# Mamba scan kernel: the reverse direction's convolution diagonals move to ScalarE, the gated product behind the fourth scan

## The chip, the cores and the metric

The kernel runs on one core of one Trainium2 chip. The metric is the device time of one execution in microseconds (us). Before the change the median of three runs is 1444.02 us (1441.96 to 1447.98).

Engine names are those of the profile: PE is TensorE's matrix multiply and PEld its weight load, DVE is VectorE, ACT is ScalarE, POOL is GpSimd, and SP is SyncE, which here issues most of the DMA transfers. A line L685 is line 685 of the kernel before, unless the text says otherwise.

## The reference, cut to what matters

The input x has 2 sequences of 1024 tokens and 256 channels. A projection with low-rank additions (mixed per sequence by `cond_8`) feeds a bidirectional Mamba layer with 512 inner channels and 16 states; a masked projection and a mixture of experts (8 experts, the best 2 for each token) follow.

```python
def _selective_scan(x, dt, Bm, Cm, A, D):
    dA = jnp.exp(dt[..., None] * A)
    dBx = (dt * x)[..., None] * Bm[:, :, None, :]
    def step(h, inputs):
        dA_t, dBx_t, C_t = inputs
        h = dA_t * h + dBx_t
        y = jnp.einsum('bdn,bn->bd', h, C_t)
        return (h, y)
...
    return jnp.swapaxes(ys, 0, 1) + x * D[None, None, :]

def _mamba_dir(h, in_proj_w, conv_w, conv_b, x_proj_w, dt_proj_w, dt_proj_b, A_log, D, out_proj_w):
    xz = h @ in_proj_w.T
    x, z = (xz[..., :D_INNER], xz[..., D_INNER:])
    x = jax.nn.silu(_causal_depthwise_conv(x, conv_w, conv_b))   # 4 taps a channel
    x_dbl = x @ x_proj_w.T
    dt = jax.nn.softplus(x_dbl[..., :DT_RANK] @ dt_proj_w.T + dt_proj_b)
    Bm = x_dbl[..., DT_RANK:DT_RANK + D_STATE]
    Cm = x_dbl[..., DT_RANK + D_STATE:]
    A = -jnp.exp(A_log)
    y = _selective_scan(x, dt, Bm, Cm, A, D)
    y = y * jax.nn.silu(z)
    return y @ out_proj_w.T
out_fwd = _mamba_dir(hidden_states, ...)          # weights _f
out_rev = _mamba_dir(h_rev, ...)                  # weights _r, reversed time
x = x + out_fwd + jnp.flip(out_rev, axis=1)
x = x + ffn(cond2(x))                             # top-2 mixture of experts
```

## The kernel before

**Stages.** Channels lie on the 128 partitions, tokens along the free dimension. A short start loads weights and prepares the first block (up to 48.5 us in the profile), the scan stage runs to about 1010 us, and the mixture of experts fills the rest.

**Blocks and periods.** The scan stage has 8 blocks, each one sequence, one direction and one chunk of 512 tokens. Their order is, for each of the two sequences, forward chunk 0, forward chunk 1, reverse chunk 1, reverse chunk 0. Blocks 0, 1, 4 and 5 are forward, blocks 2, 3, 6 and 7 reverse. The direction turns from forward to reverse behind blocks 1 and 5 and back behind block 3. A block has 16 periods, counted from 0 in each block; a period handles 32 channels x 16 states, that is 128 partitions (32 channels x 4 groups of states) times 4 scans of 512 tokens.

One period j does this, and the order on each engine is the order in which the program writes it:

- DVE makes the injection dt·x·B into a new tile `hb` of 128 x 2048 (L1517; in a block's first period in four pieces, the other three at L1549), then four scans in place (L668). Blocks 0, 2, 4 and 6 start from zero, the odd ones from a saved state. `hb` has four buffers.
- ACT makes the decays exp(dt·A), one of 128 x 512 for each scan (L642). They lie in two PSUM banks, so a decay is written two scans ahead.
- POOL multiplies the whole tile with C (L685), behind the fourth scan; in even blocks it copies the end state first (L682).
- PE adds up the states (`add_states`, folds of L711): each even period it folds the two tiles before it into the bank `yp` (there is one). Ahead of a new group of four periods it writes D·x into that bank (L700) and, in reverse blocks, adds the forward direction's result (L704).
- When `yp` holds 128 channels it is taken: by ACT as a plain copy in forward blocks (L733), in reverse blocks by DVE as a product with the gate silu(z), the gated product (L731). That is so in periods 5, 9 and 13, and in period 1 of the block that follows; the very last one is behind the loop.
- In period 15 PE spreads the next block's B rows over the partitions (`broadcast_b`, L609) into a tile of four banks of which there is one. It stands in PE's order ahead of that period's other work, and the next block's injections read it.

**Background steps.** While block i is scanned, block i+1 is prepared, one step at a time, some pieces per period. For each of the four groups of 128 channels d: the input projection's xp (evicted by ACT, L359) or the gate's sz (L382), the convolution as four matrix products with diagonal weights `cdiag` (L406, evicted by ACT at L415 and turned into silu by ACT and POOL), then the projection to dt, B and C (L452), then for each d the step `delta`: a product on PE (L493), six ACT operations (L513 to L528), four on POOL (ev L531, av L534, dt L537, u L540), and two DMA writes of the rows dt and u by SP (L543, L546). SP reads these rows back for a period, spread over partitions, two periods ahead (L630). In one period ACT gets at most four of these operations ahead of its decays (`ACT_CAP`) and up to two more late in the period, POOL at most two (`POOL_CAP`), placed ahead of that period's product with C.

**The diagonals.** `cdiag` holds 16 diagonals of 128 x 128 (4 groups of channels x 4 taps), for one direction at a time: `ident` times a tap per channel (L162, `conv_diagonals`). POOL makes the first 16 in the start. When the direction of the prepared block's successor differs, the 16 of the other direction are made anew, once the last convolution of this direction is through: in blocks 0, 2 and 4. They are put behind the POOL work of the last convolution step, four at a time (one function call counts as one operation toward `POOL_CAP`):

```python
if i + 1 < nblk and order[i + 1][1] != rev:
    out[-1]["pool"] += [partial(conv_diagonals, 1 - rev, d) for d in range(KI)]
```

**The gated product's place.** In the loop over the four scans s = 0 to 3 (L1549 and on) the gated product of a reverse block is written behind the second scan, `if s == 1 and ("vec", j) in takes`; routing work and the output projection's addition to x go behind the third and fourth.

Of the kernel before, what the change touches and what calls it, by code (L numbers as in the profile page):

```python
# [13 lines left out]
AF = mybir.ActivationFunctionType  # L14
# [7 lines left out]
DI, NS, DTR, DC = 512, 16, 16, 4  # L22
# [3 lines left out]
KI = DI // P  # L26
# [6 lines left out]
NG = NS // NI  # L33
# [15 lines left out]
def bimamba_moe_kernel(  # L49
# [23 lines left out]
    nc = tc.nc  # L73
# [3 lines left out]
    ident = const.tile([P, P], F32, name="ident")  # L77
# [38 lines left out]
    dirs = []  # L116
    for tag, (conv_w, conv_b, xprojT, dtprojT, dt_b, a_log, d_skip) in (("f", dir_f), ("r", dir_r)):
        dirs.append(
            dict(
                conv_w=mconst.tile([P, KI, DC], F32, name=f"conv_w_{tag}"),  # L120
# [5 lines left out]
                d=mconst.tile([P, KI], F32, name=f"d_{tag}"),  # L126
# [31 lines left out]
    cdiag = mconst.tile([P, KI, DC, P], F32, name="cdiag")  # L158

    def conv_diagonals(rev, d):  # L160
        for k in range(DC):
            nc.gpsimd.tensor_scalar(  # L162
                cdiag[:, d, k, :], ident, dirs[rev]["conv_w"][:, d, k : k + 1], None, ALU.mult
            )


    own = dict(reuse_waits="tile")
# [158 lines left out]
    order = []  # L326
    for b in range(B):
        order += [(b, 0, c) for c in range(NCH)] + [(b, 1, c) for c in reversed(range(NCH))]
    nblk = len(order)
# [10 lines left out]
    def step(product, act=(), hold=1, vector=(), pool=(), then=()):  # L340
        return dict(
            product=product,
            act=list(act),
            hold=hold,
            vector=list(vector),
            pool=list(pool),
            then=list(then),
            ready=lambda: True,
        )
# [40 lines left out]
    def steps_prepare(i, spares={}):  # L390

        b, rev, c = order[i]
# [4 lines left out]
        out = []  # L397
# [23 lines left out]
        def silu(v, tag, counts=0):  # L421


            box = {}

            def act1():
                box["e"] = small.tile([P, TC], F32, tag=tag, name=f"silu_{tag}_{nm}")
                nc.scalar.activation(box["e"], v, AF.Exp, scale=-1.0)

            def act2():  # L430
                nc.scalar.activation(box["e"], box["e"], AF.Ln, bias=1.0)

            def act3():
                nc.scalar.activation(box["e"], box["e"], AF.Exp, scale=-1.0)

            def multiply():
                nc.gpsimd.tensor_tensor(v, v, box["e"], ALU.mult)
                blk["gated"] = blk.get("gated", 0) + counts

            return [act1, act2, act3], multiply  # L440

        def also(st, acts, multiply):
            st.setdefault("also", []).append(step(None, acts, pool=[multiply]))

        def x_proj():
            box = {}
# [114 lines left out]
        if i:  # L561

            tags = ("ev", "u", "av", "dt")
            for d, tag in enumerate(tags):
                acts, multiply = silu(xc[:, d, :], tag, 1)
# [2 lines left out]
                if rev and d in (1, 2):  # L568
                    also(out[d], *silu(szs[i][:, d - 1, :], tags[d - 1]))
            out[-1]["hold"] = len(out[-1]["act"])  # L570
        if i + 1 < nblk and order[i + 1][1] != rev:
            out[-1]["pool"] += [partial(conv_diagonals, 1 - rev, d) for d in range(KI)]
        out.append(x_proj())
        if rev:
            for d in (2, 3):
                also(out[-1], *silu(szs[i][:, d, :], tags[d]))
        out += [delta(d, spares.get(d)) for d in range(KI)]
        return out

    def step_out(i, m):  # L580

# [35 lines left out]
    def spread(j):  # L617

        i, g = divmod(j, NQ)
        rows = blocks[i]["rows"]  # L620
        assert blocks[i].get("written", 0) > g // NI, (i, g)
        out = []
        for w, tag in enumerate(("dt4", "dtx4")):
            t = ring.tile([P, TC], F32, tag=tag, name=f"{tag}_{j}")
            if j < 2 * AHEAD:

                for k in range(NI):
                    nc.sync.dma_start(t[ts(k, QW)], rows[w, ts(g, QW), :])
            else:
                nc.sync.dma_start(  # L630
                    t, rows[w, ts(g, QW), :].unsqueeze(0).to_broadcast([NI, QW, TC])
                )
            out.append(t)
        spreads[j] = out
# [589 lines left out]
    for m in FIRST_TURN:  # L1224
# [6 lines left out]
    spares = {  # L1231
        d: pair.tile([P, 4, TC], F32, tag=tag, name=f"first_dt_{d}") for d, tag in ((2, "c4"), (3, "sz"))
    }
# [4 lines left out]
    for d in FIRST_TURN[:-1]:  # L1238
        for k in range(DC):
            taps, tap = xp[:, d, ds(k, TC)], w["conv_w"][:, d, k : k + 1]  # L1240
# [223 lines left out]
    act_q, pool_q, vec_q, takes, sp_q = [], [], [], {}, {}  # L1464
# [23 lines left out]
    def next_act(j):  # L1488
        nonlocal held
        f, frees, st = act_q.pop(0)  # L1490
        f()
        held -= frees
        if st:
            after_act(j, st)
# [8 lines left out]
    for j in range(total):  # L1503
        mark = len(traced)
        i, g = divmod(j, NQ)
        if j == max(START, i * NQ):
            steps += background(i)

        for f in sp_q.pop(j, ()):
            f()  # L1510
        if j + AHEAD < total:
            spread(j + AHEAD)
        more = extra.pop(j, dict(sp=[], act=[], pe=[], vector=[], pool=[]))
        for f in more["sp"]:
            f()
        injects = inject(j)
        injects.pop(0)()  # L1517

        if ("act", j) in takes:
            act_q.insert(0, (takes.pop(("act", j)), False, None))  # L1520
        for _ in range(min(ACT_CAP, len(act_q))):
            next_act(j)
        late = [partial(next_act, j)] * min(2, len(act_q))
        for f in more["act"]:
            f()

        if g == NQ - 1 and i + 1 < nblk:
            broadcast_b(i + 1)
        if steps and (not steps[0] or not held and steps[0]["ready"]()):
            st = steps.pop(0)  # L1530
            if st:
                begin(st)
        if more["pe"]:
            late = [f() for f in more["pe"]]
        if j and g % 2 == 0:
            add_states((j - 2, j - 1))
            i0, g0 = divmod(j - 2, NQ)
            if g0 % NI == NI - 2:
                rev0 = order[i0][1]
                takes["vec" if rev0 else "act", j + 1 if rev0 else j + 2] = partial(  # L1540
                    take, i0, g0 // NI
                )
        if j + KD >= total:
            last_out(j + KD - total, range(KI - 1))

        for s in range(NG):
            scan(j, s)
            if injects:
                injects.pop(0)()  # L1549

            if s >= NG - 2 and late:
                late.pop(0)()
            decay(j + (s + 2) // NG, (s + 2) % NG)
            if s == 1 and ("vec", j) in takes:
                takes.pop(("vec", j))()
            elif s == NG - 2:
                for f in more["vector"]:
                    f()
            elif s == NG - 1 and vec_q:
                vec_q.pop(0)()  # L1560
                held -= 1
        if rest:
            act_q[0:0] = [(rest_product(n), False, None) for n in ("mm", "yp")]

        for f, st in [pool_q.pop(0) for _ in range(min(POOL_CAP if j else 2 * POOL_CAP, len(pool_q)))]:
            f()
            if st:
                after_pool(j, st)
        for f in more["pool"]:
            f()  # L1570
        readout(j)
        pin(mark)
# [293 lines left out]
```

## Time and profile before

| | |
|---|---|
| median of the runs | 1444.02 us (1441.96 to 1447.98) |
| profiled execution, its own time | 1445.72 us |
| its span, first to last instruction | 1443.9 us |
| mean granted TensorE clock | 0.88 |
| busy PE | 1166.0 us (81 %) |
| busy DVE | 1251.9 us (87 %) |
| busy ACT | 671.9 us (47 %) |
| busy POOL | 966.5 us (67 %) |

Busy time by stage, in us (the row of the scan stage is shown with the prediction):

| stage | PE | DVE | ACT | POOL | granted clock | DMA share |
|---|---|---|---|---|---|---|
| start, 0 to 48.5 | 39.53 | 28.95 | 20.18 | 19.27 | 0.88 | 0.45 |
| experts, 1010 to 1443.9 | 413.75 | 314.97 | 69.05 | 98.41 | 0.99 | 0.71 |

How to read the views: a group of instructions has its line, engine, operation, output <- inputs, shape and count, then its busy time, the mean of one in ns, and the idle time of its engine just before them with what ended most of it. A timeline row has start, duration, engine, line and operation, and in brackets the wait before it and what released it. The costliest groups of the whole run:

```profile
L685 POOL TENSOR_TENSOR hb<-hb,c 128x2048 f32<-128x2048 f32 x127 | 576.0, 4536 | 61.7 <-DVE hb L668 52.7
L711 PE MATMUL yp<-hb,fold 128*32 128x512 f32 x1024 | 308.7, 694 | 68.7 <-POOL hb L685 68.6
L668 DVE TENSOR_TENSOR_SCAN hb<-da,state,hb 128x512 f32<-128x512 f32 x256 | 310.5, 1267 | 8.5 <-DVE hb L1517 0.5
L668 DVE TENSOR_TENSOR_SCAN hb<-da,hb 128x512 f32<-128x512 f32 x256 | 294.8, 1206 | 13.4 <-ACT da L642 5.3
L1517 DVE TENSOR_TENSOR hb<-dtx,b 128x2048 f32<-128x2048 f32 (+1 forms) x128 | 277.3, 2166 | 22.6 <-PE b L609 6.4
```

The first injections of the eight blocks start at 48.53, 165.34, 280.81, 402.40, 522.83, 643.20, 758.96 and 874.78 us.

### The profile page before, as it was taken

The numbers are of one execution on the slowest core, as the hardware profiler recorded it, in microseconds if no ns is written. First come the engines' busy times: TensorE is split into PE (matmuls) and PEld (weight loads), VectorE is DVE, ScalarE is ACT, GpSimd is POOL, SyncE is SP. The second block draws the span as 40 slices with busy tenths as digits, with TensorE's granted clock in tenths as the row PEclk, the third lists the DMA queues.
The fourth block names the chain that finished last, engine by engine and source line by source line (L and its number), as shares of the span: only waits on it lengthen the run. The fifth ranks groups of instructions, "written<-read, shape, count | busy, mean of one in ns | idle before, by whom it ended". The sixth has DMA issues, their size and how long they took to land.

```text
span 1443.9 us, 12413 instructions
## 1 busy us (share of the span) xinstructions
PE 1166.0 (81%) x3362; PEld 494.1 (34%) x3362; DVE 1251.9 (87%) x1479; ACT 671.9 (47%) x1078; POOL 966.5 (67%) x580
## 2 busy tenths in 40 slices
PE   7786776776787788677679668657999999999995
PEld 4421221221232122122123223221465656555564
DVE  6799899998999999989999998998376888888882
ACT  3666676676655665657766673332311111111110
POOL 3599998999996897999898897687222222222221
PEclk9798788798799799889778877877999999999998
DMA  5543322322322322232232244325688887921697
GB/s 146 137 126 114 108 108 77 123 106 81 106 107 72 116 104 80 84 125 90 89 130 88 82 149 152 107 91 193 217 282 287 274 289 247 313 40 22 209 336 246
DMA packets 121623, 211.32 MB, mean 146 GB/s; under 512 B 14928, under 2 KB 60240, under 8 KB 120528
## 3 DMA queue, kind: packets, MB, share of 16 engines
q1 hardware_dynamic: 110176, 199.78, 40.9%
q0 software_dynamic: 7200, 9.97, 3.4%
q10 hardware_dynamic: 4176, 0.77, 0.3%
q8 instruction: 27, 0.44, 0.1%
q14 instruction: 44, 0.36, 0.1%
HBM read 212.45 MB, written 29.49 MB: 168 GB/s over the span
## 4 chain that ended last, share of the span: by engine, by line
PE 36%; DVE 32%; POOL 21%; issue 7%; ACT 1%; DMA 1%; SPq 1%; DVEq 0%; POOLq 0%; ACTq 0%
DVE hb L668 19%; POOL hb L685 13%; PE pA L1582 9%; DVE hb L1517 9%; PE pB L1582 9%; PE pO L1661 8%; PE yp L711 4%; POOL cdiag L162 2%; PE b L609 1%; POOL ev L531 1%; PE pX L763 1%; POOL dt L537 1%; POOL u L540 1%; POOL av L534 1%; DMA yrows<-y,index 1%
## 5 line engine op out<-in xcount | busy, mean ns | idle before, releaser
L685 POOL TENSOR_TENSOR hb<-hb,c 128x2048 f32<-128x2048 f32 x127 | 576.0, 4536 | 61.7 <-DVE hb L668 52.7
L711 PE MATMUL yp<-hb,fold 128*32 128x512 f32 x1024 | 308.7, 694 | 68.7 <-POOL hb L685 68.6
L668 DVE TENSOR_TENSOR_SCAN hb<-da,state,hb 128x512 f32<-128x512 f32 x256 | 310.5, 1267 | 8.5 <-DVE hb L1517 0.5
L668 DVE TENSOR_TENSOR_SCAN hb<-da,hb 128x512 f32<-128x512 f32 x256 | 294.8, 1206 | 13.4 <-ACT da L642 5.3
L1517 DVE TENSOR_TENSOR hb<-dtx,b 128x2048 f32<-128x2048 f32 (+1 forms) x128 | 277.3, 2166 | 22.6 <-PE b L609 6.4
L642 ACT ACTIVATE da<-dt,a_r 128x512 f32<-128x512 f32 x256 | 176.0, 689 | 191.5 <-DVE hb L668 191.4
L1665 POOL DMA_INDIRECT yrows<-y,index x37 | 59.4, 1605 | 288.5 <-ACT y L1663 275.2
L642 ACT ACTIVATE da<-dt,a_f 128x512 f32<-128x512 f32 x256 | 176.4, 690 | 139.0 <-DVE hb L668 137.3
L1647 DVE STREAM_TRANSPOSE hT<-h 32x256 f32<-32x256 f32 x480 | 208.8, 435 | 6.2
L711 PEld LDWEIGHTS yp<-hb,fold 128*32 128x32 f32 x1024 | 68.0, 124 | 307.5 <-issue 167.4
L406 PE MATMUL pcv<-xp,cdiag 128*128 128x512 f32 x224 | 111.3, 642 | 26.7 <-ACT xc L415 15.9
L1586 DVE TENSOR_TENSOR h<-h,pB 128x512 f32<-128x512 f32 x73 | 50.0, 685 | 76.6 <-PE pB L1582 76.5
L1585 ACT ACTIVATE h<-pA 128x512 f32<-128x512 f32 x73 | 43.6, 597 | 146.4 <-PE pA L1582 146.3
L1663 ACT COPY y<-pO 128x256 f32<-128x256 f32 x37 | 13.8, 373 | 177.8 <-PE pO L1661 177.8
L1582 PE MATMUL pA<-w,xs 128*128 128x512 f32 x192 | 90.5, 593 | 0.2 <-DVE xs L1627 0.2
L1582 PE MATMUL pB<-w,xs 128*128 128x512 f32 x192 | 90.2, 592 | 0.0
L1661 PE MATMUL pO<-w,hT 128*128 128x256 f32 x384 | 86.9, 379 | 0.0
L334 PE MATMUL pz<-xT,in_eff 128*128 128x512 f32 x64 | 46.1, 860 | 39.9 <-ACT ev L516 39.9
L406 PEld LDWEIGHTS pcv<-xp,cdiag 128*128 128x128 f32 x224 | 43.0, 202 | 95.7 <-issue 48.3
L1661 PEld LDWEIGHTS pO<-w,hT 128*128 128x128 f32 x384 | 71.2, 190 | 9.2 <-issue 0.5
L531 POOL TENSOR_TENSOR ev<-ev,u 128x512 f32<-128x512 f32 x29 | 36.8, 1269 | 26.0 <-ACT u L528 26.0
L1582 PEld LDWEIGHTS pB<-w,xs 128*128 128x128 f32 x192 | 36.5, 190 | 45.9 <-issue 45.9
(337 smaller groups left out, 1506.5 us busy)
## 6 DMA issues: line engine op xcount, KB each, us to landing
w<-in_w_dram SPq DMA_DIRECT2D x78, 1024.0 KB
dt<-rows SPq DMA_DIRECT2D x124, 256.0 KB
dtx<-rows SPq DMA_DIRECT2D x124, 256.0 KB
xp<-in_w_dram SPq DMA_DIRECT2D x24, 1024.0 KB
in_eff<-in_w_dram SPq DMA_DIRECT2D x12, 1024.0 KB
c<-crow SPq DMA_DIRECT2D x32, 256.0 KB
rows<-dt SPq DMA_DIRECT2D x29, 256.0 KB
rows<-u SPq DMA_DIRECT2D x29, 256.0 KB
```

The source lines that it names most:

```text
L406: nc.tensor.matmul(box["ps"], cdiag[:, d, k, :], xp[:, d, ds(off, TC)], start=(k == 0), stop=(k == DC - 1),)
L531: nc.gpsimd.tensor_tensor(box["ev"], box["ev"], box["u"], ALU.subtract)
L642: nc.scalar.activation(da, spreads[j][0], AF.Exp, scale=a[:, g, s : s + 1])
L668: nc.vector.tensor_tensor_scan(h_s, das.pop((j, s))[:, ::turned], h_s, 0.0 if i % NCH == 0 else states[b, rev][:, g, s : s + 1], ALU.mult, ...
L685: nc.gpsimd.tensor_tensor(hb, hb, blocks[i]["c4"], ALU.mult)
L711: nc.tensor.matmul(yp[ts(q, QW), :], fold, hbs[j][:, s, :], start=False, stop=(s == NG - 1), tile_position=(0, q * QW), skip_group_check=True,
L1517: injects.pop(0)()
L1582: nc.tensor.matmul(ps, xs[:, k, :], w_sb[:, k, ts(n, TC)], start=(k == 0), stop=(k == KD - 1))
L1586: nc.vector.tensor_tensor(h, h, pb, ALU.mult)
L1647: nc.vector.transpose(hT[ts(k, QW), :, ts(i, QW)], hk[ts(i, QW), :, ts(k, QW)])
L1661: nc.tensor.matmul(po, hT[:, k, :], w2_sb[:, k, :], start=(k == 0), stop=(k == KH - 1))
L1665: nc.gpsimd.indirect_dma_start(out=yrows, out_offset=bass.IndirectOffsetOnAxis(ap=index_of[ph][:, k : k + 1], axis=0), in_=y, in_offset=No ...
```

## The change

Two edits. The 48 diagonals of the three turns are no longer made by POOL with a multiplication but by ACT, as an activation (identity function, the tap as its scale per channel). They no longer follow the last convolution: four of them are put into ACT's order with the step `delta` of the same d, as an additional step that begins in the same period as that `delta`'s product and is queued behind its six operations. The 16 diagonals of the start stay on POOL. And the gated product of reverse blocks is written behind the fourth scan of its period rather than behind the second; the third scan's routing work is no longer an alternative to it. `also` takes any number of POOL operations now, none included, and is called with none for the diagonals.

```diff
+    def turn_diagonals(rev, d):
+        for k in range(DC):
+            tap = dirs[rev]["conv_w"][:, d, k : k + 1]
+            nc.scalar.activation(cdiag[:, d, k, :], ident, AF.Identity, scale=tap)
...
-        def also(st, acts, multiply):
-            st.setdefault("also", []).append(step(None, acts, pool=[multiply]))
+        def also(st, acts, *pool):
+            st.setdefault("also", []).append(step(None, acts, pool=pool))
...
-        if i + 1 < nblk and order[i + 1][1] != rev:
-            out[-1]["pool"] += [partial(conv_diagonals, 1 - rev, d) for d in range(KI)]
         out.append(x_proj())
...
-        out += [delta(d, spares.get(d)) for d in range(KI)]
-        return out
+        deltas = [delta(d, spares.get(d)) for d in range(KI)]
+        if i + 1 < nblk and order[i + 1][1] != rev:
+            for d in range(KI):
+                also(deltas[d], [partial(turn_diagonals, 1 - rev, d)])
+        return out + deltas
...
-            if s == 1 and ("vec", j) in takes:
+            if s == NG - 1 and ("vec", j) in takes:
                 takes.pop(("vec", j))()
-            elif s == NG - 2:
+            if s == NG - 2:
                 for f in more["vector"]:
                     f()
             elif s == NG - 1 and vec_q:
```

In the built kernel each turn's diagonals stand on ACT four at a time, ahead of a period's third decay (its first two are written in the period before). The periods are 13 and 15 of block 0 and 1 and 3 of block 1; 10, 12 and 14 of block 2 and 0 of block 3; 10, 12 and 14 of block 4 and 0 of block 5. The eviction of the step that follows (sz, L382, or xp, L359) stands behind them. The orders of PE and SP are the same as before. On POOL 48 instructions are gone, and one product of a gate's silu stands one period earlier in block 2.

## The prediction

> **What bounds the kernel now.** The busy time by stretch comes first. Columns: PE, PEld, DVE, ACT and POOL busy us with counts, granted TensorE clock, DMA share, GB/s.
>
> ```profile
> 48.50:1010.00 961.50, 712.77 (x1825) 222.01 (x1824) 908.02 (x730) 582.69 (x920) 848.81 (x471) 0.83 0.33 109
> ```
>
> In the scan stage DVE works 908 of 961.5 us and POOL 849: two engines close to full in one loop, and each can hold the other. The time that a change can win here is DVE's idle time, so I read next what DVE waits for (total us, times, longest).
>
> ```profile
> DVE ysum L731 <- PE yp L711: 9.8, 5, 3.9
> ...
> DVE hb L668 <- ACT da L642: 5.6, 6, 2.3
> ```
>
> Five gated products (L731) wait 9.8 us for TensorE's folds. In the timeline they start at 354.88, 385.85, 505.11, 888.31 and 986.35, after waits of 3.88, 2.86, 1.93, 0.48 and 0.69 us. The other eleven wait for nothing.
>
> For what the diagonals do, I read the chain of waits around the first turn of direction (start, us, what).
>
> ```profile
> 127.98 3.50 POOL cdiag L162 x6
> ...
> 138.76 4.53 POOL hb L685
> 143.29 1.22 POOL ev L531
> ...
> 153.38 4.57 POOL hb L685
> 157.95 0.04 issue
> 158.00 3.62 PE yp L711 x14
> 161.62 2.34 PE b L609 x5
> ...
> 165.34 0.70 DVE hb L1517
> ```
>
> Sixteen diagonals put POOL behind, its products with C stay late, TensorE's fold of periods 12 and 13 waits for product 13, the new block's B row waits behind the fold in TensorE's order, and DVE's first injection of block 1 waits for B. In the timeline injections stand 6.85 us apart (120.45, 127.30, 134.15, 141.00); from 141.00 on that puts block 1 at 161.55. It starts at 165.34: 3.8 us lost.
>
> **The change, part by part.** *Removed from POOL:* 48 diagonals, 16 at each of three turns (blocks 0, 2 and 4).
>
> ```profile
> L162 POOL TENSOR_SCALAR cdiag<-ident,conv_w_r 128x128 f32<-128x128 f32 x32 | 18.7, 606 | 0.0
> ```
>
> 48 x 0.606 = 29.1 us of POOL work go. That is not the gain: each turn wins only until the next thing in the loop is late.
>
> Turn 1 (block 0). POOL's next step, ev of the first dt, starts at 143.25 behind the late product. Its input u ends on ACT at 140.66 + 0.61 = 141.27, and ev stands before product 12 in POOL's order. So POOL can come forward by at most 143.25 - 141.27 = 2.0 us. From there to the end of product 13 it works without a pause, so product 13 ends at about 156.0 instead of 157.94. Fold and B keep their 7.4 us (157.94 to 165.34): block 1 starts at about 163.4. Gain 1.9 of the 3.8.
>
> Turn 3 (block 4) is the same with a longer delay:
>
> ```profile
> 593.93 0.61 ACT L528 ACTIVATE u<-u 128x512 f32<-128x512 f32 x1
> ...
> 597.68 1.28 POOL L531 TENSOR_TENSOR ev<-ev,u 128x512 f32<-128x512 f32 x1
> ```
>
> u is there at 594.54 and POOL takes it at 597.68, right behind product 8, itself late by the diagonals at 574.19, 581.25 and 590.62. Forward by 3.1 us; product 13 (end 634.31), fold, B and DVE's first injection of block 5 (643.20) follow. DVE's stalls on the way there (1.8 us each at 596.15 and 618.63) go too, but are contained in this: POOL's product 13 sets the end. Gain 3.1.
>
> Turn 2 (block 2) meets the second edit.
>
> ```profile
> 348.33 4.66 POOL L162 TENSOR_SCALAR cdiag<-ident,conv_w_f 128x128 f32<-128x128 f32 x8
> ...
> 348.41 6.43 PE L711 MATMUL yp<-hb,fold 128*32 128x512 f32 x14 [5.49 <-POOL hb L685]
> ...
> 354.88 0.69 DVE L731 TENSOR_TENSOR ysum<-sz,yp 128x512 f32<-128x512 f32 x1 [3.88 <-PE yp L711]
> ...
> 357.89 0.67 ACT L642 ACTIVATE da<-dt,a_r 128x512 f32<-128x512 f32 x1
> 358.50 0.61 ACT L528 ACTIVATE u<-u 128x512 f32<-128x512 f32 x1
> ...
> 359.02 0.67 ACT L359 ACTIVATE xp<-px,in_bias 128x512 f32<-128x512 f32 x1
> ...
> 361.36 0.69 ACT L642 ACTIVATE da<-dt,a_r 128x512 f32<-128x512 f32 x1 [1.67 <-DVE hb L668]
> ```
>
> *Moved:* the gated product, from behind the second scan to behind the fourth. Two scans are 2 x 1.21 us in even blocks and 2 x 1.27 in odd ones; that much more wait is hidden. Behind it on DVE now stands the next injection, where the third and fourth scan and POOL's product stood. Without the diagonals and with the product moved, period 9 of block 2 (injection 346.30) runs through: fourth scan over at 353.2, product at once, next injection at 353.9 instead of 357.74. From there POOL is the bound, with 2 x 1.27 + 4.53 + 0.2 and gaps = 7.3 us a period against DVE's 6.85: products 9 to 13 end at 358.1, 365.7, 373.1, 380.4 and 387.8 (product 13 before: 394.21). The wait at 385.85 is gone as well: the fold of product 11 starts at 373.1 and takes at most the 6.4 us seen, done at 379.5, and scan 13 ends at 381.4. TensorE's way into block 3 then counts from its xp eviction, 0.8 us behind injection 14 and now behind four diagonals: fold from 389.0, 3.8 + 3.7 us of fold and B, block 3 at 396.6 instead of 402.40. Gain 5.8; I take 5.7.
>
> Block 3, period 13: the wait of 1.93 us goes, and its product with C no longer stands behind the gated product's 0.6 us. POOL's ev there waits for ACT, which follows DVE, so the whole train moves: 2.5. Block 7: 0.48 in period 1; in period 13 0.69 for DVE, and up to 1.4 because product 13 heads TensorE's last chain (994.13 to 1009.2): I take 1.0. The eleven products that waited for nothing gain nothing: their 0.67 us moves from before the third scan to before the next injection, in the same DVE sum.
>
> *Added to ACT:* four activations of 128x128 with each dt, twelve times. No row has that form; the nearest of ACT's groups (busy us, mean ns, idle before) are
>
> ```profile
> L642 ACT ACTIVATE da<-dt,a_r 128x512 f32<-128x512 f32 x256 | 176.0, 689 | 191.5 <-DVE hb L668 191.4
> ...
> L528 ACT ACTIVATE u<-u 128x512 f32<-128x512 f32 x29 | 17.8, 615 | 0.1
> ...
> L148 ACT ACTIVATE a_r<-a_r 128x64 f32<-128x64 f32 x1 | 0.2, 243 | 0.0
> ```
>
> From below, the 128x64 row (243 ns); from above, the 128x512 row with a scale per channel (689). Between 243 at 64 and 615 at 512 the line gives 0.30 at 128, and a per-channel scale adds 689 - 615 = 0.07; neighbours overlap by 0.1 (L513 and L516 start 0.57 apart and take 0.67). Four cost about 1.15 us; the ends are 0.9 and 2.5. They stand before an eviction (sz or xp), in the gap between the second decay of a period and its third, which waits for the first scan. In the window above that gap has 1.67 us left, the least of the twelve (also at 159.48), and the third decay may be another 0.5 late (a scan of 1.2 less a decay of 0.69). So 1.15 us costs DVE nothing; at 2.5 it would cost 2.5 - 2.2 = 0.3, twelve times 0.3 = 4 us. The evicted bank comes free 1.15 us later for TensorE's next dt product, which ACT reads a period later; only turn 2 pays for it, as counted. SP and TensorE issue the same instructions in the same order, and the rows of dt and u go out when POOL is done, so not later than before.
>
> The Trainium skill (ScalarE: Activation LUTs, What ACT_TABLE_LOAD costs) gives 186 ns + 0.833 ns an element and 93 ns for each pointer operand, and has neighbours overlap by 93 ns. With the scale alone as a pointer that makes four of 386 ns less three overlaps, 1.27 us. By it the sum stays, since 1.27 is under the 1.67 as well; no run here shows that form yet.
>
> **Sum.** 1.9 + 5.7 + 3.1 + 2.5 + 0.5 + 1.0 = 14.7 us, against the profiled execution: span 1443.9, its own time 1445.72, the median of three runs 1444.02 (1441.96 to 1447.98), 0.1% apart. 1444.0 - 14.7 = 1429.3. What follows the scan stage starts earlier by that much and keeps its length.
>
> **Rivals.**
> *All waits go* (1421): the turns' ends run through as well. With unstalled injections block 3 starts at 395.8 and block 5, seven periods of 6.85 behind 587.43, at 635.4: 3.8 + 6.6 + 7.8 + 2.5 + 0.5 + 1.4 = 22.6. For it: turns 1 and 3 keep 1.9 and about 4.8 us of delay in my count. Part of it is a slow TensorE: the 14 folds above took 6.43 us after 5.49 idle, while 16 took 3.63 with no idle before them (305.42). With folds and B always at the fast rate, turn 3 ends (5.12 - 3.6) 1.5 us sooner and turn 2 about 0.9. The rest would need POOL to get u earlier. Against: u follows DVE's scans whatever POOL does. The Trainium skill (TensorE: Matmul & The Clock Gate, Part 1) says that half rate follows an idle window of about 3.4 us; the trace agrees with the 6.43.
> *Little of it stays* (1437): only four of the gated products' waits go for good (3.88 + 1.93 + 0.48 + 0.69 = 7.0 us), because POOL's 7.3 us a period makes up the lag again by the block's end. For it: the lag grows 0.46 a period even without diagonals. Against: in blocks 0 and 4 there are only 4 to 7 such periods.
> *Slower* (1452): a gated product that ends two scans later frees the yp bank later, and TensorE stands in order before the diagonal product of D (L700). Decisive is whether that delays the fold. The bank is free 0.67 us after the fourth scan; L700 and L704 take 1.97 + 1.91 at their slowest (360.79): 4.55 us. The fold needs POOL's product, at least 0.14 + 4.53 = 4.67 us after that scan. By 0.1 us it holds. If TensorE is later than that, each of the 15 moved products can pass on up to its two scans, 2.4 us, by way of the buffers of hb that the fold gives back; from 1.0 us each the 14.7 are gone, and at 1.5 the sum is 1444.0 - 14.7 + 22.5. Against: TensorE waits for the gated product only 1.1 us in all before (L700), with the bank busy to the same event.
> *No effect*: excluded as far as instructions go; the built order shows 48 diagonals moved and 15 products behind the fourth scan, with no table load added.
>
> **How the numbers follow.** Forecast 1429.3 with chance 0.56 (own range 1425 to 1433: 4 us up for diagonals at 2.5 us, 1.5 us down a turn for the fold's rate), all waits gone 0.18, little stays 0.15, slower 0.11, since its margin is only 0.1 us. The range 1419 to 1441, 2 us beyond the first and 4 beyond the second neighbour, leaves out the slower case and about a quarter of these two. 0.5% of 1444 is 7.2 us, about what a measurement tells from nothing: faster below 1436.8. That holds for the first two cases and almost half of the third: 0.81; same 0.08; slower 0.11.
>
> **What would show it.** Right: POOL's cdiag rows down from 64 to 16; ACT's of 128x128 at 0.3 to 0.4 us; no DVE wait of L731 for L711 over 0.5 us; POOL's ev of the first dt in blocks 0 and 4 waiting for ACT's u; blocks 1, 3 and 5 starting about 2, 8 and 13 us earlier (turn 3 adds to the 10 before it); L668 waiting for L642 no more than 6 us. Wrong: that last wait up by 4 us or more, or L700 waiting for L731 with later folds behind it.

## The result and the profile after

The changed kernel takes 1434.43 us (median of four runs, 1432.22 to 1435.06), the kernel before beside it 1444.84 us. The ratio is 0.9922, with a 95% interval of 0.99 to 0.9944: 10.4 us, faster by 0.8%. The profiled execution's span went from 1443.9 to 1433.1 us. The forecast was 1429.3, with 1425 to 1433 as its own range and 1419 to 1441 as the wider one: the time lies in the wider range, and 1.4 us above the narrower.

In the table of what DVE waits for (total us, times, longest), the gated product (now L738) is gone; the same table of before had it with 9.8 us in five waits. What is left in the scan stage are the starts of blocks, which wait for the B rows (L616) or for what POOL does beside them, and the decays as before (5.6 us):

```profile
DVE hb L1524 <- PE b L616: 7.3, 2, 5.3
...
DVE hb L675 <- ACT da L649: 5.6, 7, 1.9
...
DVE hb L1524 <- POOL state L689: 2.5, 1, 2.5
```

The groups of POOL and of ACT show the diagonals on their new engine. The 16 of the start stayed on POOL; the 48 others take 387 ns each on ACT against 606 on POOL:

```profile
L162 POOL TENSOR_SCALAR cdiag<-ident,conv_w_f 128x128 f32<-128x128 f32 x16 | 9.6, 619 | 2.3 <-DMA conv_w_f<-in_conv_w_f_dram 2.3
...
L169 ACT ACTIVATE cdiag<-ident,conv_w_r 128x128 f32<-128x128 f32 x32 | 10.1, 388 | 0.0
...
L169 ACT ACTIVATE cdiag<-ident,conv_w_f 128x128 f32<-128x128 f32 x16 | 5.0, 386 | 0.0
```

To see where the time came from, subtract the start of each block's first injection after from the same start before (before: 48.53, 165.34, 280.81, 402.40, 522.83, 643.20, 758.96, 874.78 us):

| block | 0 | 1 | 2 | 3 | 4 | 5 | 6 | 7 |
|---|---|---|---|---|---|---|---|---|
| start after, us | 48.07 | 162.38 | 277.02 | 393.17 | 511.81 | 631.39 | 747.88 | 860.70 |
| gained so far | 0.5 | 3.0 | 3.8 | 9.2 | 11.0 | 11.8 | 11.1 | 14.1 |
| gained so far, second profile | 1.1 | 3.4 | 4.5 | 10.1 | 11.8 | 12.6 | 12.0 | 12.0 |

The second profile is of another execution of the same changed kernel (the first experiment). The 14.0 us that the first profile has gained by block 7's end shrink again in the first expert tiles, where TensorE ran at half its clock for part of the time (granted clock 0.66 from 1000 to 1010 us, 1.00 in the same stretch of work before).

At turn 3, this is the chain of waits after the change (start, us, what):

```profile
616.89 4.53 POOL hb L692
621.47 5.32 PE yp L718 x14
626.79 4.51 PE b L616 x8
631.30 3.73 PE pz L339 x4
635.79 5.59 PE pcv L411 x8
```

The chain before had these rows there:

```profile
634.36 5.12 PE yp L711 x14
639.48 3.64 PE b L609 x8
```

The B rows took 3.64 us before and 4.51 now, and the two products behind them 3.73 and 5.59, where they take 1.98 and 3.70 at full clock. So part of what POOL won went to a slower TensorE. At turn 2 it is the timeline of ACT and TensorE that shows it:

```profile
376.44 0.67 ACT L649 ACTIVATE da<-dt,a_r 128x512 f32<-128x512 f32 x1
...
377.05 1.26 ACT L169 ACTIVATE cdiag<-ident,conv_w_f 128x128 f32<-128x128 f32 x4
...
378.22 0.67 ACT L364 ACTIVATE xp<-px,in_bias 128x512 f32<-128x512 f32 x1
378.94 2.07 PE L498 MATMUL pt<-xdbl,dtprojT_r 16*128 16x512 f32 x2 [4.41 <-ACT xp L364]
...
380.94 2.08 PE L707 MATMUL yp<-xc,ddiag_r 128*128 128x512 f32 x2
...
384.65 4.80 PE L718 MATMUL yp<-hb,fold 128*32 128x512 f32 x16
```

TensorE stands idle for 4.41 us until ACT has evicted xp, which stands behind four diagonals. Then it starts at half rate: 2.07 and 2.08 us for products that took 1.12 and 1.70 before, 4.80 for folds that took 3.85. Before, the same stretch was:

```profile
390.19 1.12 PE L493 MATMUL pt<-xdbl,dtprojT_r 16*128 16x512 f32 x2 [2.46 <-ACT xp L359]
391.24 1.70 PE L700 MATMUL yp<-xc,ddiag_r 128*128 128x512 f32 x2
...
394.57 3.85 PE L711 MATMUL yp<-hb,fold 128*32 128x512 f32 x16
```

### The profile page after: what moved, and what is told of

Same layout as the page of the kernel before. It is cut to its first block, busy times and chain, and to the rows that moved or that the text cites. A ratio compares the mean times of both kernels' runs of the same rounds, so it can differ in the third digit from the quotient of the medians.

```text
span 1433.1 us, 12413 instructions
## 1 busy us (share of the span) xinstructions
PE 1173.5 (82%) x3362; PEld 499.0 (35%) x3362; DVE 1252.7 (87%) x1479; ACT 685.0 (48%) x1126; POOL 939.3 (66%) x532
## 4 chain that ended last, share of the span: by engine, by line
DVE 40%; PE 36%; POOL 13%; issue 5%; DMA 3%; ACT 2%; SPq 1%; DVEq 0%; ACTq 0%; POOLq 0%
DVE hb L675 25%; DVE hb L1524 12%; PE pA L1589 9%; PE pB L1589 9%; POOL hb L692 8%; PE pO L1668 8%; PE yp L718 2%; PE pcv L411 2%; PE b L616 1%; POOL ev L536 1%; POOL dt L542 1%; POOL u L545 1%; PE pz L339 1%; PE pX L770 1%; POOL av L539 1%
## 5 line engine op out<-in xcount | busy, mean ns | idle before, releaser
L718 PE MATMUL yp<-hb,fold 128*32 128x512 f32 x1024 | 298.8, 680 | 39.7 <-POOL hb L692 39.6
L411 PE MATMUL pcv<-xp,cdiag 128*128 128x512 f32 x224 | 114.5, 658 | 21.2 <-ACT xc L420 12.9
L339 PE MATMUL pz<-xT,in_eff 128*128 128x512 f32 x64 | 48.5, 900 | 41.7 <-ACT ev L521 41.7
```

The source lines that it names most:

```text
L339: nc.tensor.matmul(ps, in_eff[:, b, k, ts(m, P)], xT[:, k, cols], start=(k == 0), stop=(k == KD - 1))
L411: nc.tensor.matmul(box["ps"], cdiag[:, d, k, :], xp[:, d, ds(off, TC)], start=(k == 0), stop=(k == DC - 1),)
L718: nc.tensor.matmul(yp[ts(q, QW), :], fold, hbs[j][:, s, :], start=False, stop=(s == NG - 1), tile_position=(0, q * QW), skip_group_check=True,
```

## The experiments

All times are medians; the kernel before, in the same sessions, had 1444.7 to 1445.4. Edits are shown against the changed kernel if nothing else is said.

**The changed kernel again.** No edit.

> The changed kernel once more, for a second profile. If the change takes only the waits that the first profile shows, the ratio is 0.992 to 0.994 again. The first profile's ledger also has gains and losses of 0.8 to 3 us at places where the two kernels issue the same work and TensorE runs at another clock (start of block 2 +0.8, block 4 -1.5, block 7 +2.1, first expert tiles -2.4). If those are chance, they sit elsewhere or have another sign in this profile, and the three turns and periods 13 of blocks 3 and 7 keep theirs within 0.5 us. If the change causes them, all come back.

Measured: 1432.86 us (1425.33 to 1433.65), ratio 0.9887 (0.9854 to 0.9921). All eight runs together have a median of 1433.5, and that is what the others are held against. The turns came back: from period 9 of the block to the next block's start, turn 1 gained 1.7 and 1.5 us (first and second profile), turn 2 4.4 and 4.5, and period 13 of block 3 2.06 and 2.07. What came back otherwise is the gain at the start of block 2 (+0.8 and +1.1) and the loss at the start of block 4 (-1.4 both times; the B rows ahead of it took 4.53 us, and with the 3.70 us that they take in evict_first, below, this loss is gone). What did not come back: block 7's start (+3.0 and +0.6) and the first expert tiles (-2.4 and +0.6). So these last two are chance. The run of 1425.33 us had a granted clock of 0.887, the others 0.867 to 0.869.

**One edit each.** diag_only has the diagonals on ACT and the gated product behind the second scan; move_only has the product behind the fourth and the diagonals on POOL.

```diff
diag_only
-            if s == NG - 1 and ("vec", j) in takes:
+            if s == 1 and ("vec", j) in takes:
                 takes.pop(("vec", j))()
-            if s == NG - 2:
+            elif s == NG - 2:
move_only
+        if i + 1 < nblk and order[i + 1][1] != rev:
+            out[-1]["pool"] += [partial(conv_diagonals, 1 - rev, d) for d in range(KI)]
         out.append(x_proj())
...
-            for d in range(KI):
-                also(deltas[d], [partial(turn_diagonals, 1 - rev, d)])
```

> Diagonals on ACT, the gated product still behind the second scan. Theory A (POOL's lateness at the turns is the main loss, and the moved product only takes the waits of blocks 3 and 7 and a rest in block 2): POOL is on time in block 2, so its first gated product there waits under 0.5 us; the waits of block 3 period 13 (1.9) and block 7 (0.5 + 0.7) stay, and period 13 of block 2 keeps 0 to 1: 3 to 4 us of the 10.4 are not won, time 1437 to 1439. Rival B (the gain comes from the moved product): 1442 to 1445.

> The gated product behind the fourth scan, the diagonals still on POOL. Theory A: turns 1 and 3 stay as before; in block 2 POOL sets the pace, its product 13 ends about 1.2 us earlier than before; 2.1 in block 3 and 0.9 in block 7 are won: 4 us, time 1440 to 1442. Rival B: the waits of 9.8 us before the gated product go and stay gone: 1434 to 1436.

Measured: diag_only 1432.79 us, ratio 0.9911 (0.9878 to 0.9944); move_only 1442.79 us, ratio 0.9978 (0.9961 to 0.9994). The moved product alone brings 2.6 us, less than the 4 of theory A and far from rival B's 9 to 11, so rival B falls: the diagonals are the larger part. diag_only was expected at 1437 to 1439 and came out like the full change. In its waits the gated product stands with only this:

```profile
DVE ysum L738 <- PE yp L718: 1.1, 3, 0.6
```

With POOL on time, most of the 9.8 us of waiting went without the move. Period 13 of block 3 gained 1.34 us here, against 2.06 with the move. The runs of diag_only spread from 1429.07 to 1437.80, so whether the move brings anything on top was not settled here; evict_no_move below asks again.

**What the diagonals cost on ACT.** no_turn leaves them out on every engine, double makes each of them twice.

```diff
no_turn
-            for d in range(KI):
-                also(deltas[d], [partial(turn_diagonals, 1 - rev, d)])
double
+            for _ in range(2):
+                nc.scalar.activation(cdiag[:, d, k, :], ident, AF.Identity, scale=tap)
```

> The changed kernel without the 48 turn diagonals on any engine: the convolutions of later directions then use the first direction's taps; all else is the same. Theory A (the diagonals on ACT are hidden but for the xp eviction ahead of the third block's start, 1.26 us late): 1.3 us less than the changed kernel, about 1433. Rival C (ACT's decays pass the diagonals on to DVE): 12 times 0.3 to 1.2, so 4 us or more less, under 1430.5. Rival D (wholly hidden): no difference, within 0.5 us.

> Every turn diagonal is made twice on ACT: 8 x 0.387 less overlaps = 2.5 us with each dt instead of 1.27, which is the upper end of the predicted cost. Theory A (slack of 1.67 before the third decay plus 0.5 of its own lead): 0.3 us for DVE in each of the 12 periods at most, and the xp eviction ahead of block 3 another 1.26 late: 1.3 to 5 us over the changed kernel, 1434.5 to 1438.5. Rival B (ACT's time passes on to DVE in full): 12 x 1.26 = 15 us, 1448. Rival C (hidden in full): 1433.5.

Measured: no_turn 1431.03 us, ratio 0.9886 (0.9863 to 0.9909), 2.5 us under the changed kernel, between theory A's 1.3 and rival C's 4. Its profile has 1.8 us of that where theory A put it: the last period of block 2 took that much less (the B rows before block 3 end earlier). Another 1.4 us are in period 4 of block 2, where no diagonals stand; turn3_first, below, has them too with all its diagonals. DVE's waits for decays are 3.8 us in five, against 5.6 in seven, and the five stand at the same places as in the changed kernel: none of them is the diagonals' doing.

double has 1434.46 us, ratio 0.9928 (0.9915 to 0.994), 0.9 us over the changed kernel, which is within the spread of the runs. Rival B (15 us) falls. The profile still shows a price at 2.5 us with each dt. Waits for decays rose from 5.6 to 8.4 us:

```profile
DVE hb L676 <- ACT da L650: 8.4, 13, 1.6
```

Eight of the thirteen are new and stand in periods with diagonals; they are 3.9 us together, from 0.2 to 0.8 us each. That is the 4 us that the prediction had for this price, though in eight periods of the twelve, and in four of them at twice its 0.3 or more. The last period of block 2 is 1.7 us longer as well. Gains elsewhere, 1.7 us in the last period of block 4 among them, hide this in the median.

**The eviction ahead of the diagonals.** evict_first lets waiting diagonals step behind the next eviction.

```diff
+        turn = [a for a in act_q if getattr(a[0], "func", None) is turn_diagonals]
+        for a in turn:
+            act_q.remove(a)
         for one in [st, *st.get("also", ())]:
             for k, f in enumerate(one["act"]):
                 frees = one is st and k < st["hold"]
+                if not frees:
+                    act_q.extend(turn)
+                    turn = []
                 act_q.append((f, frees, one if k == len(one["act"]) - 1 else None))
+        act_q.extend(turn)
```

> Each four diagonals one step later in ACT's order, behind the eviction of sz or xp that they stood ahead of. Theory A (of the diagonals on ACT only the delayed eviction before block 3 costs anything; without them block 3 started 1.8 us earlier from period 15 on): the loss of 2.5 to 2.9 us at the start of block 3 goes down to about 0.8; time 1.3 to 1.9 us under the changed kernel's 1433.5 (its eight runs together), 1431.5 to 1432.2. Rival B (that gain was chance of the clock): start of block 3 as before, 1433 to 1434.

Measured: 1429.75 us (1426.94 to 1430.16), ratio 0.9894 (0.988 to 0.9908), 3.7 us under the changed kernel and below theory A's 1431.5 to 1432.2. The timeline of the same stretch (block 2, period 14):

```profile
376.90 0.67 ACT L364 ACTIVATE xp<-px,in_bias 128x512 f32<-128x512 f32 x1
377.47 1.26 ACT L169 ACTIVATE cdiag<-ident,conv_w_f 128x128 f32<-128x128 f32 x4
...
377.62 1.12 PE L498 MATMUL pt<-xdbl,dtprojT_r 16*128 16x512 f32 x2 [2.00 <-ACT xp L364]
...
381.95 4.23 PE L718 MATMUL yp<-hb,fold 128*32 128x512 f32 x16
```

TensorE waits 2.00 us in place of 4.41, stays at full rate for its first product, and begins the folds at 381.95 in place of 384.65; period 15 is 2.6 us shorter. That is 1.3 for the eviction itself and as much again for the clock. Block 3's first period gives 0.7 us back: there the diagonals stand between a late xp and the decays, and a scan waits 0.85 us for ACT. The 1.9 that stay are what no_turn won there. Which change made the rest of the median's 3.7 us is open; the profile has gains of 0.8 to 1.2 us around the starts of blocks 4 and 5, where the B rows took 3.70 in place of 4.5 us.

**POOL's product ahead of ev.** product_first writes POOL's product with C ahead of ev and av in every period that begins a dt; both adds evict_first to it.

```diff
+        product_first = bool(pool_q) and getattr(pool_q[0][0], "__name__", "") == "add1"
+        if product_first:
+            readout(j)
         for f, st in [pool_q.pop(0) for ...
             f()
...
-        readout(j)
+        if not product_first:
+            readout(j)
```

> In the periods where POOL begins a dt (ev, av), its product with C is written ahead of them instead of behind, so that it no longer waits for ACT's u. Theory A (POOL's 2.2 to 2.8 us of waiting for u, then 7.3 us a period, is what still makes the ends of turns 1 and 3 late): product 13 of block 4 ends 2.4 us earlier and block 5 starts 2 to 2.5 us earlier; in turn 1 TensorE's fold starts at its D product anyway (154.5), so 0.3; in turn 2 TensorE waits for the xp eviction, 0. Time about 2.5 us under the changed kernel: 1430.5 to 1431.5. Rival B (TensorE at half rate takes it: fold and B stretch as they start earlier): under 0.5 us, 1433 to 1434.

> The two edits together. Theory A: the gains add, 4 to 4.5 us under the changed kernel, 1429 to 1430, which is 15 to 16 us under the kernel before. Rival B: as the better of the two alone or the changed kernel itself, 1431.5 to 1434.

Measured: 1439.11 us, ratio 0.9966 (0.995 to 0.9983), and 1439.94 us, ratio 0.9966 (0.9954 to 0.9978): 5.6 and 6.4 us slower than the changed kernel. Both theories fall for the whole kernel. The timeline of product_first shows why:

```profile
58.27 4.54 POOL L692 TENSOR_TENSOR hb<-hb,c 128x2048 f32<-128x2048 f32 x1 [0.19 <-POOL state L689]
...
62.77 1.27 POOL L536 TENSOR_TENSOR ev<-ev,u 128x512 f32<-128x512 f32 x1
...
66.82 1.26 POOL L545 TENSOR_TENSOR u<-dt,xc 128x512 f32<-128x512 f32 x1
...
92.41 2.29 DVE L1524 TENSOR_TENSOR hb<-dtx,b 128x2048 f32<-128x2048 f32 x1 [3.70 <-DMA dtx<-rows]
```

In block 0 the dt rows of the block itself are still being made, and the next periods read them at once. Behind the product POOL finished them late (this u's row is written at 68.11 us, in the changed kernel at 58.39), they reached DVE late, and by period 5 the kernel was 7.5 us behind the changed one. Another 2.8 us went in period 8 of block 2, where ACT waited 3.82 us for TensorE's projection (L457) with the decays queued behind that, so the rows were not the cause there. At turn 3, though, both gained 3.8 to 4.2 us from period 15 of block 4 to block 5. So:

**The same in block 4 alone**, with evict_first.

```diff
-        product_first = bool(pool_q) and getattr(pool_q[0][0], "__name__", "") == "add1"
+        product_first = bool(pool_q) and getattr(pool_q[0][0], "__name__", "") == "add1" and i == 4
```

> evict_first, and POOL's product with C ahead of ev and av in block 4 alone (the third turn). Theory A (product_first lost its time by rows of dt and u that came late in blocks 0 and 2, and its 3.8 to 4.2 us at the start of block 5 are real): block 4's rows are needed late enough, so block 5 starts 2.4 to 4 us earlier and nothing is lost elsewhere: 1426 to 1427.5. Rival B (those 4 us were only POOL's slack from the earlier stalls of 11 us): under 0.5 us, 1429.3 to 1430.

Measured: 1425.58 us (1424.18 to 1426.85), ratio 0.9861 (0.9846 to 0.9876), 4.2 us under evict_first and 19.8 us (1.4%) under the kernel before: faster than both kernels of this case. POOL's timeline at the first dt, evict_first and then turn3_first:

```profile
581.00 1.28 POOL L536 TENSOR_TENSOR ev<-ev,u 128x512 f32<-128x512 f32 x1 [2.22 <-ACT u L533]
...
583.83 4.52 POOL L692 TENSOR_TENSOR hb<-hb,c 128x2048 f32<-128x2048 f32 x1
```

```profile
581.01 4.52 POOL L692 TENSOR_TENSOR hb<-hb,c 128x2048 f32<-128x2048 f32 x1
585.49 1.27 POOL L536 TENSOR_TENSOR ev<-ev,u 128x512 f32<-128x512 f32 x1
```

POOL starts its product 2.8 us earlier and finds u ready afterwards. Product 13 ends at 615.05 instead of 617.65, 2.6 us earlier; the folds take 3.62 instead of 5.32 (next experiment). Together they account for the 4.1 us by which block 5 starts earlier. The two profiled executions are only 2.1 us apart in all, because that of evict_first was its fastest; other places lost up to 2.2 us and gained up to 1.4.

**The gated product's place again**, on top of evict_first: back behind the second scan (the edit of diag_only).

> evict_first with the gated product back behind the second scan. With the diagonals off POOL, diag_only showed only three waits of 1.1 us in all ahead of the gated product. Theory A (the move is worth just these waits): 0.5 to 1.5 us over evict_first's 1429.8, so 1430.3 to 1431.3, with the loss in period 13 of blocks 3 and 7. Rival B (with the product behind the fourth scan TensorE waits 6.4 to 7.3 us for it ahead of the D product, against 1.1 without the move; this and what it does to TensorE's clock take the gain back): 1428.5 to 1429.8. Rival C (the prediction's sum, 4.0 us for blocks 3 and 7): 1433 to 1434.

Measured: 1434.33 us (1431.55 to 1435.69), ratio 0.9922 (0.9908 to 0.9935), 4.6 us over evict_first: the number of rival C. Period 13 of block 3 has the wait again, and the loss there is 2.2 us:

```profile
494.22 0.69 DVE L738 TENSOR_TENSOR ysum<-sz,yp 128x512 f32<-128x512 f32 x1 [2.06 <-PE yp L718]
```

Its two other waits of this kind are 0.71 us in period 1 of block 4 and 0.31 in period 9 of block 6, where the periods are 0.8 and 0.4 us longer. So about 3.4 of the 4.6 us belong to waits of this product, and theory A, which counted 1.1, falls. diag_only, with the product in the same place, waited just 0.59 us in period 13 of block 3. TensorE's folds ahead of it make the difference, in evict_no_move first, then in diag_only:

```profile
487.64 6.54 PE L718 MATMUL yp<-hb,fold 128*32 128x512 f32 x14 [3.46 <-POOL hb L692]
```

```profile
490.54 5.06 PE L718 MATMUL yp<-hb,fold 128*32 128x512 f32 x14 [3.84 <-POOL hb L692]
```

POOL freed the folds 4.5 us before DVE came to the gated product in both; 6.54 less 5.06 is 1.48 us, and the waits differ by 1.47. So the wait that the move hides is as long as the folds are slow, and at the full rate of 3.62 us there would be none. The rest of what evict_no_move lost is 1.7 us in the last period of block 3, where the B rows took 4.79 us against 3.70 in evict_first, and 1.6 at the start of block 3; gains elsewhere offset part of it, and one profile can't tell whether the move or the clock's phase made these.

**TensorE kept busy.** busy_pe issues the D product two more times (the bank begins anew each time, so the sum is the same) in TensorE's wait before the last folds of block 4; turn3_busy puts them on turn3_first. Against evict_first and turn3_first:

```diff
-            nc.tensor.matmul(
-                yp, w["ddiag"][:, d, :], xc[:, d, :], start=True, stop=False, skip_group_check=True
-            )
+            for _ in range(3 if (i, d) == (4, KI - 1) else 1):
+                nc.tensor.matmul(
+                    yp, w["ddiag"][:, d, :], xc[:, d, :], start=True, stop=False, skip_group_check=True
+                )
```

> evict_first with the D product of block 4's last group of periods issued three times in place of once (each begins the bank anew, the sum is the same): about 2 us more work for TensorE in the 2.8 us in which it waits for POOL's product 13. Theory A (TensorE's clock falls to half behind idle time, and that makes the 14 folds behind it take 5.32 instead of 3.6 us): the folds take 3.6 to 4.2, block 5 starts 1.2 to 1.7 us earlier, time 1428 to 1428.7. Rival B (the clock there follows something else, such as the mean load of a longer stretch): folds at 5.3 again, time 1429.8. Rival C (the extra products run at half clock themselves and outlast the wait): block 5 later by up to 1.2 us, 1431.

> turn3_first and busy_pe together. Both act on the same stretch: turn3_first's 14 folds behind product 13 already take 3.62 us, and TensorE waits only 1.61 us there, so the extra D products (1.7 us) have nothing left to win. Theory A (busy_pe's 4.6 us under evict_first are 1.7 us of faster folds and chance): block 5 starts as in turn3_first or up to 0.5 us later, time 1425 to 1426.5. Rival B (the extra products win more than the folds show, by a clock that stays up behind them): 1421 to 1423.5.

TensorE's timeline in evict_first, then in busy_pe:

```profile
612.77 1.13 PE L707 MATMUL yp<-xc,ddiag_f 128*128 128x512 f32 x2
613.83 1.04 PE L718 MATMUL yp<-hb,fold 128*32 128x512 f32 x2
617.71 5.32 PE L718 MATMUL yp<-hb,fold 128*32 128x512 f32 x14 [2.84 <-POOL hb L692]
```

```profile
611.82 2.84 PE L708 MATMUL yp<-xc,ddiag_f 128*128 128x512 f32 x6
614.59 1.04 PE L719 MATMUL yp<-hb,fold 128*32 128x512 f32 x2
616.73 3.62 PE L719 MATMUL yp<-hb,fold 128*32 128x512 f32 x14 [1.09 <-POOL hb L692]
```

1.7 us more work make the folds 1.70 us faster, and period 15 of block 4 is 1.72 us shorter: for the folds it is theory A, shown by adding work and nothing else. The granted clock in these stretches of two us says the same (columns: us, PE busy, clock, DMA share, GB/s); evict_first:

```profile
616.00:618.00 2.00, 0.29 (x2) 1.00 0.26 87
618.00:620.00 2.00, 2.00 (x8) 0.52 0.38 140
```

busy_pe:

```profile
616.00:618.00 2.00, 1.27 (x6) 1.00 0.29 107
618.00:620.00 2.00, 2.00 (x10) 1.00 0.53 197
...
624.00:626.00 2.00, 2.00 (x3) 0.50 0.26 100
```

The last row shows what the folds alone don't: the clock falls six us later instead, where evict_first has 1.00. The gate's input projection (L339) there takes 3.68 us in place of 1.98, ACT evicts it later, four diagonals stand behind that eviction, and a scan in block 5's first period waits for the decays behind both:

```profile
630.08 1.28 DVE L675 TENSOR_TENSOR_SCAN hb<-da,state,hb 128x512 f32<-128x512 f32 x1 [1.39 <-ACT da L649]
```

That period is 1.29 us longer, so 0.4 of the 1.72 us stay.

busy_pe took 1425.17 us, ratio 0.9857 (0.9842 to 0.9872), 4.6 us under evict_first: more than the 1.7 that the folds explain. turn3_busy took 1426.38 us, ratio 0.987 (0.9853 to 0.9886): the extra products win nothing where the folds already take 3.62, as theory A had it. They did not keep the clock up there either. TensorE had waited 3.56 us ahead of them, and the six ran at half clock in part:

```profile
610.47 4.54 PE L708 MATMUL yp<-xc,ddiag_f 128*128 128x512 f32 x6
```

The profiled execution of evict_first was its fastest (1426.94), and against it busy_pe's profiled execution gained just 1.65 us, 0.4 of it at this turn. So busy_pe shows what makes the folds slow; where the 4.6 us of its median come from stays open.

## Why the prediction was right, point by point

**What bounds, and the turns.** The working of the turns held to about half a us up to TensorE's folds. The times below are compared after taking off what the profile had gained before that turn (1.30, 4.87 and 9.85 us):

| step | predicted | less the earlier gain | measured |
|---|---|---|---|
| turn 1: ev waits for u, starts at | 141.27 | 139.97 | 140.04 |
| turn 1: product 13 ends | 156.0 | 154.7 | 154.73 |
| turn 1: block 1 starts | 163.4 | 162.1 | 162.38 |
| turn 2: product 13 ends | 387.8 | 382.9 | 382.67 |
| turn 2: folds start | 389.0 | 384.1 | 384.65 |
| turn 2: block 3 starts | 396.6 | 391.7 | 393.17 |
| turn 3: ev starts | 594.54 | 584.69 | 584.77 |
| turn 3: product 13 ends | 631.2 | 621.4 | 621.42 |
| turn 3: block 5 starts | 640.1 | 630.3 | 631.39 |

The step that was mis-sized is the last one in turns 2 and 3. The prediction put "3.8 + 3.7 us of fold and B" behind turn 2, and kept before's 5.12 and 3.64 behind turn 3. They took 4.80 + 3.70 and 5.32 + 4.51, and at turn 2 the products ahead of the folds were slow as well. So turn 2 won 4.4 in place of 5.7. Turn 3 won 2.0 up to block 5's start and 1.2 with its first two periods, in place of 3.1. That is 3.2 of the 4.3 us by which the gain of 10.4 stays behind the 14.7; the product's move, below, lacks another 1.1. The places that the prediction named gave 10.1 us. That the whole came out at 10.4 is luck in part: other places gained up to 3.0 and lost up to 2.4 us, and in the first profile, with 10.8 in all, they nearly cancel, while the second gained 12.3.

**The product's move.** Predicted 2.5, 0.5 and 1.0 us for period 13 of block 3 and periods 1 and 13 of block 7. Measured 2.06, nothing (the period got 1.1 us longer in one profile, 0.2 in the other) and 0.84. That the waits go was right (no gated product waits any more); that they need the move was right for block 3, but its worth there is 0.7 us against diag_only and 2.2 against evict_no_move, depending on how slow the folds are. For block 2 the move did nothing that POOL on time had not done: diag_only gains the same 3.0 us in period 13 there.

**ACT.** Four activations were put at 1.15 us, with ends of 0.9 and 2.5. They take 1.26 to 1.28. The Trainium skill (ScalarE: Activation LUTs, What ACT_TABLE_LOAD costs) makes it 1.27 by its formula, and the trace agrees with 386 to 388 ns each. That they cost DVE nothing held, and double shows the margin. At the upper end, 2.5 us, its 4 us were about right (3.9 in double). "Only turn 2 pays for it, as counted" held in the place, but not in the size: without diagonals (no_turn) the period is 1.8 us shorter, and with the eviction first 2.6, of which the next period takes 0.7 back. The later eviction leaves TensorE idle for longer, and the products behind it run at half rate. Not all of that half rate is the diagonals' doing: in no_turn TensorE still waits 2.54 us there, and its folds take 4.56.

**The rivals.** "All waits go" (1421) did not come, for the reason given against it: POOL waits 2.2 us for u in both turns. turn3_first, with evict_first in it, comes within 5 us of its time by letting POOL do its product in that wait. "Little of it stays" (1437) is nearer to the measured time than the forecast is, 2.6 us against 5.1, but its mechanism fell: the gained time was still there at each next block. Blocks 1, 3 and 5 start 3.0, 9.2 and 11.8 us earlier, where about 2, 8 and 13 were forecast. "Slower" named the right place. TensorE does wait longer for the gated product: 7.3 us in three waits after the change, 1.1 before. But POOL's product is still later, so the fold does not move:

```profile
975.51 1.12 PE L707 MATMUL yp<-xc,ddiag_r 128*128 128x512 f32 x2 [3.19 <-DVE ysum L738]
...
980.14 3.62 PE L718 MATMUL yp<-hb,fold 128*32 128x512 f32 x14 [1.67 <-POOL hb L692]
```

TensorE waits 3.19 us for DVE, and afterwards still 1.67 us for POOL. Behind the other two waits (1.52 and 2.63 us) it waits 2.20 and 1.18 us more for POOL. So the margin was 1.2 to 2.2 us, wider than the 0.1 of the prediction, which had the products ahead of the fold at their slowest.

## What to carry to other kernels

Work taken off an engine that is late wins only up to the next input it has to wait for: follow the chain to that input (here ACT's u) before counting busy time, and then let the engine do something else in that wait, as turn3_first does. When work is put onto an engine with room, look at what stands behind it in that engine's order rather than at its load: the diagonals made no decay late, but the eviction behind them held TensorE. Test such an order change where it is wanted only: the same reordering lost 5.6 us in all blocks and won 4.2 in one. And follow a gain one step past the place where it was made: here the next period took back 1.29 of 1.72 us in busy_pe and 0.7 of 2.6 in evict_first.

## What the runs showed of the hardware

TensorE's clock fell to half after a wait of 2.84 us between busy stretches (evict_first, granted clock 0.52 from 618 us on), and 1.7 us of repeated work in that wait kept it at 1.00 for the folds, up to a fall to 0.50 at 624 us. The Trainium skill (TensorE: Matmul & The Clock Gate, Part 1) names an idle window of about 3.4 us as what brings half rate; here a shorter wait was enough, so the measurement decides. The length of the wait alone doesn't settle it, though: in the changed kernel waits of 2.63 us (up to 439.02) and 3.19 us (up to 975.51) were followed by a granted clock of 1.00 and products at 1.12 us.

The same 8 matmuls for the B rows took 3.70 us at full clock and up to 4.88 us where it fell (busy_pe, 850.31), and 8 of the convolution 3.70 against 5.69 (turn3_first, 625.98); both stand at the starts of blocks, where DVE waits for them. Single places (block 7's start, the first expert tiles) moved by 2.4 and 3.0 us between two executions of one kernel.
